# A selective-scan loop in a fixed order, and its output products as seven block products

## The chip, the cores and the metric

The kernel runs on one core of a Trainium2 chip. The metric is the device time of one execution in microseconds (us). A core has five engines with a queue each: TensorE (PE in the profile; its weight loads are listed as PEld), VectorE (DVE), ScalarE (ACT), GpSimd (POOL) and SyncE (SP), which here issues the DMAs. Each engine works through its own queue in order and waits on semaphores for the others.

## The reference

One layer of three parts, each on a layer norm of a residual `x` of 16 x 32 tokens with 512 features: a graph attention on 3-d coordinates, a selective scan, and a feed-forward part with low-rank additions. The change lies in the scan, which, cut to what matters, is:

```python
h = x * rsqrt(mean(x * x) + EPS) * norm_w
proj = einsum('bsd,od->bso', h, in_proj_w)            # gate 8192, hBC 8192 + 2048, dt 128
gate, hBC, dt = ...
hBC = silu(causal_conv(hBC, conv_w, conv_b))          # four taps along the sequence
hid, B, C = ...                                       # 128 heads of 64, 8 groups of 128
dt = softplus(dt + dt_bias);  A = -exp(A_log)
# within one chunk: y[i] = sum_j (C[i] . B[j]) * exp(segsum(A * dt))[i, j] * (hid * dt)[j]
y = (Y_diag + Y_off) + Dp * hid
yg = y * silu(gate)
yg = yg * rsqrt(mean over the group's 1024 channels of yg * yg + EPS) * gnorm_w
out = residual + einsum('bsd,od->bso', yg, out_proj_w)
```

All tensors of the scan are f32.

## The kernel before, in words

Three functions run one after the other: `graph_part` (up to about 1340 us of the span), `scan_part`, and `ffn_part` (from about 2276 us). Only `scan_part` is touched.

The 512 tokens lie along the free axis in four blocks of 128 (index q), channels along the partitions. The 8192 inner channels are 64 tiles of 128 (index t), eight per group (TG = 8), in 8 groups (G_M = 8). For a group g:

- `inner(g)` makes, for each of eight tiles i, the gate projection (`project`, L1177: four 512-column matmuls on `hT`, into the PSUM tag "p" with two buffers), its Silu on ScalarE (L1256, tile `gs`), the convolution projection, and `convolve`: an Identity on ScalarE that applies the last tap and the bias (L1184, tile `cy`), three taps on VectorE that read the same PSUM buffer (L1189), and the Silu into `hid` (L1192). From group 1 on it also advances `parts`, the loading and splitting of the low-rank weights of the feed-forward part into three bf16 parts (L148 to L185: masks and memsets on GpSimd, small DMAs, eight VectorE operations for each of ten pieces).
- `mix(g)` takes each tile i back to token-major order with four transposes (`pht`, L1285, PSUM tag "m", two buffers), multiplies by dt (`hd`, L1287), builds two decay matrices (`el`, L1298), multiplies on TensorE (`py`, L1306, PSUM tag "y"), adds `Dp * hid` (L1310), gates (L1311), squares on ScalarE (`ssq`, `sq`, L1313 and L1316), sums the squares on GpSimd (L1317), and scales by `gnorm_w` on ScalarE (L1318). For every second tile `decays` makes the decays of four heads: a product on GpSimd (`da`, L1265, two buffers), a matmul (`pl`, L1270, PSUM tag "m"), an Exp (`ed`, L1275).
- `close(g)` sums the squares over the group with a matmul (`pn`, L1325), takes the reciprocal root (`rstd`, L70 to L80, two ScalarE operations with other function tables), loads eight tiles of `out_proj` (`wo`, L1333, ten buffers), and for each q accumulates eight 128 x 128 x 512 matmuls (`po`, L1338, PSUM tag "o") and adds them, times the root, to the residual `xt` (L1341).

The source calls `inner(g + 1)`, `mix(g)`, `close(g)` in this order, but a scheduler decides the order on each engine: it takes instructions by priority as soon as their inputs and buffers are free. So the projections of group g + 1, the mix of g and the products of g and of the group before it are interleaved in small pieces.

An f32 matmul is two passes in the profile, each with a weight load of its own; a transpose is one pass.

Of the kernel before, what the change touches and what calls it, by code (L numbers as in the profile page):

```python
# [8 lines left out]
F32 = mybir.dt.float32  # L9
# [3 lines left out]
AF = mybir.ActivationFunctionType  # L13
ALU = mybir.AluOpType
# [4 lines left out]
P = 128  # L19
B = 16  # L20
C = 32
D = 512
# [9 lines left out]
CB = 3  # L32
# [8 lines left out]
H_M, G_M, SEQ = 128, 8, 32  # L41
D_INNER = 8192
NT = D_INNER // P
TG = NT // G_M
# [85 lines left out]
class LowRank:  # L130
# [981 lines left out]
def scan_part(nc, tc, cx, I, id32, ones, xt, u, rstd, lows):  # L1112
# [3 lines left out]
    wk = cx.enter_context(tc.tile_pool(name="swk", bufs=2))  # L1116
    sm = cx.enter_context(tc.tile_pool(name="ssm", bufs=3))
    wpool = cx.enter_context(tc.tile_pool(name="sw", bufs=4))
    ps_p = cx.enter_context(tc.tile_pool(name="sps_p", bufs=2, space=PSUM))
    ps_m = cx.enter_context(tc.tile_pool(name="sps_m", bufs=2, space=PSUM))  # L1120
    ps_y = cx.enter_context(tc.tile_pool(name="sps_y", bufs=2, space=PSUM))
    ps_o = cx.enter_context(tc.tile_pool(name="sps_o", bufs=2, space=PSUM))
# [23 lines left out]
    for t, base, cmul, op, b2, c2, s2 in ((le, 0, -1, ALU.is_ge, 0, 1, -32), (gt, 0, 1, ALU.is_gt, 31, -1, 32)):  # L1146
        nc.gpsimd.memset(t, 1.0)
        nc.gpsimd.affine_select(
            out=t, in_=t, compare_op=op, fill=0.0, base=base, pattern=[[-cmul, P]], channel_multiplier=cmul
        )  # L1150
        nc.gpsimd.affine_select(
            out=t, in_=t, compare_op=ALU.is_ge, fill=0.0, base=b2, pattern=[[s2, 4], [0, 32]], channel_multiplier=c2
# [10 lines left out]
    for q in range(4):  # L1163
        pt = ps_m.tile([P, 4, P], F32, tag="m", name=f"pt{q}")
# [6 lines left out]
    def project(t, tag):  # L1171

        w = wpool.tile([P, 4, P], F32, tag="win", name=f"win{tag}", bufs=6)
        nc.sync.dma_start(out=w, in_=I["in_proj"][t])
        pp = ps_p.tile([P, D], F32, tag="p", name=f"pp{tag}")
        for k in range(4):
            nc.tensor.matmul(pp, lhsT=w[:, k], rhs=hT[:, k], start=(k == 0), stop=(k == 3))  # L1177
        return pp

    def convolve(dst, t, tag):  # L1180

        pp = project(NT + t, f"c{tag}")
        y = wk.tile([P, B, SEQ], F32, tag="cy", name=f"cy{tag}", bufs=3)
        nc.scalar.activation(  # L1184
            y.rearrange("p b s -> p (b s)"), pp, AF.Identity, bias=cb[:, t:t + 1], scale=cw[:, t, 3:4]
        )
        pv = pp.rearrange("p (b s) -> p b s", b=B)
        for sh in (1, 2, 3):
            nc.vector.scalar_tensor_tensor(  # L1189
                y[:, :, sh:], pv[:, :, :SEQ - sh], cw[:, t, 3 - sh:4 - sh], y[:, :, sh:], ALU.mult, ALU.add  # L1190
            )
        nc.scalar.activation(dst, y.rearrange("p b s -> p (b s)"), AF.Silu)  # L1192


    wdt = wpool.tile([P, 4, P], F32, tag="win", name="wdt", bufs=6)
# [9 lines left out]
    with tc.tile_pool(name="soft", bufs=1) as sp:  # L1205
# [11 lines left out]
        s2 = sp.tile([P, 4, H_M], F32, name="s2")  # L1217
        nc.vector.tensor_tensor(s2, s, s, ALU.mult)
        acc = sp.tile([P, 4, H_M], F32, name="acc")
# [12 lines left out]
    CB = sc.tile([P, G_M, 4, P], F32, name="CB")  # L1232
# [13 lines left out]
    parts = lows.load(low)  # L1246
    big = cx.enter_context(tc.tile_pool(name="sbig", bufs=2))

    def inner(g):

        gs = big.tile([P, TG, D], F32, tag="gs", name=f"gs{g}")
        hid = big.tile([P, TG, D], F32, tag="hid", name=f"hid{g}")
        for i in range(TG):
            t = g * TG + i
            pg = project(t, f"g{t}")
            nc.scalar.activation(gs[:, i], pg, AF.Silu)  # L1256
            convolve(hid[:, i], t, f"h{t}")
            if g > 0:
                next(parts, None)
        return gs, hid  # L1260

    def decays(h):

        da = sm.tile([P, 4, 4, SEQ], F32, tag="da", name=f"da{h}", bufs=2)
        nc.gpsimd.tensor_tensor(  # L1265
            da, lei.unsqueeze(1).unsqueeze(1).to_broadcast([P, 4, 4, SEQ]),
            dA[:, :, h:h + 4].rearrange("p q h -> p h q").unsqueeze(3).to_broadcast([P, 4, 4, SEQ]), ALU.mult,
        )
        pl = ps_m.tile([P, 4, 4, SEQ], F32, tag="m", name=f"pl{h}")
        nc.tensor.matmul(  # L1270
            pl.rearrange("p h q i -> p (h q i)"), lhsT=gt, rhs=da.rearrange("p h q i -> p (h q i)"),
            start=True, stop=True,
        )
        ed = sm.tile([P, 4, 4, SEQ], F32, tag="ed", name=f"ed{h}", bufs=2)
        nc.scalar.activation(ed, pl, AF.Exp)  # L1275
        return ed

    def mix(g, gs, hid):

        ssq = wk.tile([P, D], F32, tag="ssq", name=f"ssq{g}")  # L1280
        for i in range(TG):
            t = g * TG + i
            pt = ps_m.tile([P, 4, P], F32, tag="m", name=f"pht{t}")
            for q in range(4):
                nc.tensor.transpose(pt[:, q], hid[:, i, q * P:(q + 1) * P], id32)  # L1285
            hd = sm.tile([P, 4, 2, 64], F32, tag="hd", name=f"hd{t}")
            nc.vector.tensor_tensor(  # L1287
                hd, pt.rearrange("p q (h c) -> p q h c", h=2),
                dt[:, :, 2 * t:2 * t + 2].unsqueeze(3).to_broadcast([P, 4, 2, 64]), ALU.mult,
            )  # L1290
            py = ps_y.tile([P, 4, P], F32, tag="y", name=f"py{t}")
            if i % 2 == 0:
                decay = decays(2 * t)
            els = []
            for j in range(2):

                el = sm.tile([P, 4, P], F32, tag="el", name=f"el{2 * t + j}")
                nc.vector.tensor_tensor(  # L1298
                    el.rearrange("p q (b i) -> p q b i", b=4),
                    decay[:, 2 * (i % 2) + j].unsqueeze(2).to_broadcast([P, 4, 4, SEQ]),  # L1300
                    CB[:, g].rearrange("p q (b i) -> p q b i", b=4), ALU.mult,
                )
                els.append(el)
            for q in range(4):
                for j in range(2):
                    nc.tensor.matmul(  # L1306
                        py[64 * j:64 * j + 64, q], lhsT=hd[:, q, j], rhs=els[j][:, q], start=True, stop=True
                    )
            pyf = py.rearrange("p q t -> p (q t)")
            nc.vector.scalar_tensor_tensor(hid[:, i], hid[:, i], dpc[:, t:t + 1], pyf, ALU.mult, ALU.add)  # L1310
            nc.vector.tensor_tensor(gs[:, i], gs[:, i], hid[:, i], ALU.mult)  # L1311
            if i == 0:
                nc.scalar.activation(ssq, gs[:, i], AF.Square)  # L1313
            else:
                sq = wk.tile([P, D], F32, tag="sq", name=f"sq{t}")
                nc.scalar.activation(sq, gs[:, i], AF.Square)  # L1316
                nc.gpsimd.tensor_tensor(ssq, ssq, sq, ALU.add)  # L1317
            nc.scalar.activation(gs[:, i], gs[:, i], AF.Copy, scale=gnw[:, t:t + 1])  # L1318
        return ssq

    def close(g, gs, ssq):

        pn = ps_y.tile([P, 4], F32, tag="y", name=f"pn{g}")
        for q in range(4):
            nc.tensor.matmul(pn[:, q:q + 1], lhsT=ssq[:, q * P:(q + 1) * P], rhs=ones[:, 0:1], start=True, stop=True)  # L1325
        mean = sm.tile([P, 4], F32, tag="gm", name=f"gm{g}")
        nc.vector.tensor_scalar(mean, pn, 1.0 / (TG * P), None, ALU.mult)
        rs = sm.tile([P, 4], F32, tag="gr", name=f"gr{g}")
        rstd(sm, rs, mean, 4, f"gn{g}")
        wo = []  # L1330
        for i in range(TG):
            w = wpool.tile([P, D], F32, tag="wo", name=f"wo{g}_{i}", bufs=TG + 2)
            nc.sync.dma_start(out=w, in_=I["out_proj"][g * TG + i])  # L1333
            wo.append(w)
        for q in range(4):
            po = ps_o.tile([P, D], F32, tag="o", name=f"po{g}_{q}")
            for i in range(TG):
                nc.tensor.matmul(  # L1338
                    po, lhsT=gs[:, i, q * P:(q + 1) * P], rhs=wo[i], start=(i == 0), stop=(i == TG - 1)
                )  # L1340
            nc.vector.scalar_tensor_tensor(xt[:, q], po, rs[:, q:q + 1], xt[:, q], ALU.mult, ALU.add)  # L1341

    cur = inner(0)
    for g in range(G_M):
        nxt = inner(g + 1) if g + 1 < G_M else None
        ssq = mix(g, *cur)
        close(g, cur[0], ssq)
        cur = nxt


def ffn_part(nc, tc, cx, I, id32, xt, layernorm, lows, out):
# [139 lines left out]
```

## Time and profile before

| what | value |
|---|---|
| median of 3 runs | 2381.26 us (2378.29 to 2382.47) |
| the profiled execution | 2376.64 us, span of its instructions 2374.9 us |
| TensorE matmul busy | 2172.0 us (91%), 39234 passes |
| TensorE weight loads busy | 1243.6 us (52%) |
| VectorE busy | 1694.5 us (71%) |
| ScalarE busy | 1093.6 us (46%) |
| GpSimd busy | 831.4 us (35%) |
| mean granted clock of TensorE | 0.978 |
| first gate projection, last output product | 1424.3 us, 2274.7 us |

The strips of the page cut the span into 40 slices of 59.4 us; a digit is the busy share in tenths. The scan's main loop fills slices 25 to 39. A row of the profile names the line, the engine, the operation, the tile written and the tiles read.

### The profile page before, as it was taken

To read this page: it belongs to the slowest core of one execution; us is meant where nothing else is said; L and a number is where in the kernel's file an instruction comes from. 1 tells how busy PE (TensorE), PEld (TensorE's weight loads), DVE (VectorE), ACT (ScalarE), POOL (GpSimd) and SP (SyncE) were. 2 spreads that over 40 slices of the span, in tenths; PEclk is the share of its full clock that TensorE was granted. 3 is DMA by queue.
4 is the path that set the end of the run, shared out by engine and by line. 5 is a ranking of instruction groups with operands and counts; after the bars stand their busy time and mean duration, and the time that the engine had idled before them with its cause. 6 is when DMAs were issued, how large, how long until landed. Compare 5 with 4: busy or idle time off the path is not lost. (4 is left out here: it accounts for less than half of the span.)

```text
span 2374.9 us, 88834 instructions
## 1 busy us (share of the span) xinstructions
PE 2172.0 (91%) x39234; PEld 1243.6 (52%) x39234; DVE 1694.5 (71%) x3674; ACT 1093.6 (46%) x2023; POOL 831.4 (35%) x897
## 2 busy tenths in 40 slices
PE   5598899999989988799999689999999999999979
PEld 2254555776547765477777444444444444444422
DVE  8487897998979999799899757455362635446543
ACT  6685666556755544355555233233242423333321
POOL 2155656556555566555555100021120202012200
PEclk9899999999999999999999799999999999999989
DMA  1323242231231412313111212212212031220000
GB/s 49 81 59 76 51 81 57 52 81 43 59 78 42 90 41 55 81 43 85 43 39 41 94 56 79 72 53 58 67 40 84 23 102 49 63 62 14 27 36 18
DMA packets 121625, 137.99 MB, mean 58 GB/s; under 512 B 18398, under 2 KB 79506, under 8 KB 121154
## 3 DMA queue, kind: packets, MB, share of 16 engines
q1 hardware_dynamic: 121240, 132.32, 22.6%
q8 instruction: 308, 5.05, 0.9%
q14 instruction: 77, 0.63, 0.1%
HBM read 77.02 MB, written 12.85 MB: 38 GB/s over the span
## 5 line engine op out<-in xcount | busy, mean ns | idle before, releaser
L888 POOL TENSOR_TENSOR EN<-e,rz 128x480 f32<-128x480 f32 x344 | 342.4, 995 | 509.6 <-DVE rz L886 423.1
L913 PE MATMUL u<-WA,DD 128*32 128x128 bf16 (+1 forms) x16512 | 412.5, 248 | 19.4 <-issue 19.1
L918 ACT COPY us<-u 128x512 f32<-128x512 f32 x516 | 301.9, 586 | 154.2 <-PE u L913 138.2
L913 PEld LDWEIGHTS <-DD 128*32 128x32 f16 x16512 | 337.5, 97 | 53.5 <-issue 51.1
L873 ACT ACTIVATE e<-s,smc 128x480 f32<-128x480 f32 x344 | 227.3, 661 | 270.2 <-PE s L868 243.5
L809 POOL TENSOR_TENSOR DD<-fs,crep 128x480 f16<-128x480 f32 (+2 forms) x344 | 349.4, 1016 | 0.0
L941 PE MATMUL h<-e,us 128*32 128x30 f32 (+1 forms) x11008 | 281.3, 210 | 47.1 <-DVE e L894 25.6
L941 PEld LDWEIGHTS h<-e,us 128*32 128x32 f32 (+1 forms) x11008 | 247.2, 125 | 147.0 <-issue 68.1
L1189 DVE SCALAR_TENSOR_TENSOR cyh<-ppch,t_conv_w,cyh 128x496 f32<-128x496 f32 (+2 forms) x192 | 137.5, 716 | 221.9 <-ACT cyh L1184 217.9
L860 DVE TENSOR_REDUCE c<-s 128x16 bf16<-128x480 f32 x344 | 220.0, 640 | 77.0 <-PE s L851 73.9
L1265 POOL TENSOR_TENSOR da<-lei,dA 128x512 f32<-128x512 f32 x32 | 40.6, 1269 | 612.6 <-PE pl L1270 577.6
L1338 PE MATMUL po<-wo,gs 128*128 128x512 f32 x512 | 240.5, 605 | 10.4 <-DVE xt L1341 10.3
L1177 PE MATMUL ppch<-hT,winch 128*128 128x512 f32 x512 | 232.2, 593 | 0.0
L1177 PE MATMUL ppg<-hT,wing 128*128 128x512 f32 x512 | 231.9, 593 | 0.0
L894 DVE STREAM_TRANSPOSE e<-EN 128x512 f32<-128x512 f32 x344 | 224.5, 653 | 0.0
L880 DVE TENSOR_REDUCE z<-e 128x16 f32<-128x480 f32 x344 | 219.4, 638 | 0.4 <-ACT e L873 0.4
L541 ACT ACTIVATE sgn<-kd 128x512 bf16<-128x512 f32 x256 | 153.1, 598 | 48.6 <-PE kd L540 45.7
L851 PEld LDWEIGHTS <-DD 128*32 128x32 f16 x5504 | 80.8, 96 | 156.8 <-issue 131.6
L751 DVE TENSOR_SCALAR oh<-it,rank 128x512 bf16<-128x512 f16 x512 | 156.6, 366 | 7.6 <-PE pp L705 7.5
L1177 PEld LDWEIGHTS ppch<-hT,winch 128*128 128x128 f32 x512 | 93.6, 190 | 122.7 <-issue 122.4
L851 PE MATMUL s<-DX,DD 128*32 128x120 f16 x5504 | 141.5, 222 | 16.9 <-DMA DX<-DD 15.7
L1177 PEld LDWEIGHTS ppg<-hT,wing 128*128 128x128 f32 x512 | 95.8, 190 | 114.0 <-issue 114.0
(327 smaller groups left out, 2845.5 us busy)
## 6 DMA issues: line engine op xcount, KB each, us to landing
DX<-DD SPq DMA_DIRECT2D x456, 90.0 KB
wo<-in_out_proj SPq DMA_DIRECT2D x64, 256.0 KB
wing<-in_in_proj SPq DMA_DIRECT2D x64, 256.0 KB
winch<-in_in_proj SPq DMA_DIRECT2D x64, 256.0 KB
crep<-dC SPq DMA_DIRECT2D x128, 64.0 KB
dS<-so SPq DMA_DIRECT2D x32, 256.0 KB
fs<-dS SPq DMA_DIRECT2D x128, 64.0 KB
wincB<-in_in_proj SPq DMA_DIRECT2D x8, 256.0 KB
```

The source lines that it names most:

```text
L809: nc.gpsimd.tensor_tensor(d[:, :, m0 - n0:n1 - n0], win, crep[:, :, m0:n1].unsqueeze(3).to_broadcast([P, 4, n1 - m0, K]), ALU.subtract,)
L851: nc.tensor.matmul(s[rh, j * 4 * QB:(j + 1) * 4 * QB].rearrange("p (b q) -> p b q", b=4), lhsT=d[:, h, c0:c0 + 32], rhs=dx[:, h, :, c0:c0 ...
L860: nc.vector.tensor_reduce(c, live["s", at, gi].rearrange("p (i q) -> p i q", q=QB), AX.X, ALU.max, negate=True)
L873: nc.scalar.activation(e, s.rearrange("p (i q) -> p i q", q=QB), AF.Exp, scale=smc)
L880: nc.vector.tensor_reduce(z, e, AX.X, ALU.add)
L888: nc.gpsimd.tensor_tensor(en[:, :, :QB], e, rz.unsqueeze(2).to_broadcast([P, NI, QB]), ALU.mult)
L894: nc.vector.transpose(e.rearrange("p i q -> p (i q)"), en.rearrange("p i q -> p (i q)"))
L913: nc.tensor.matmul(u[rh, jj], lhsT=d[:, h, c0:c0 + 32], rhs=WA[k][:, h].rearrange("p b o -> p (b o)"), start=(jj == 0 and k == 0), stop=(k ...
L918: nc.scalar.copy(us[:, j - jj:j + 1], u)
L941: nc.tensor.matmul(h[r:r + co, pr, q0:q0 + QB], lhsT=us[:, j, b * co:(b + 1) * co], rhs=e[:, 4 * j + b, :QB], start=npair > 1, stop=True, ...
L1177: nc.tensor.matmul(pp, lhsT=w[:, k], rhs=hT[:, k], start=(k == 0), stop=(k == 3))
L1338: nc.tensor.matmul(po, lhsT=gs[:, i, q * P:(q + 1) * P], rhs=wo[i], start=(i == 0), stop=(i == TG - 1))
```

## The change

The main loop's instructions now stand, on every engine, in the order in which the source issues them (`tc.manual_schedule()`). `inner`, `mix` and `close` are cut into steps for that: `gate`, `current` (the convolution, in two halves), and a class `Mix` with `turn` (transposes, `hd`, `el`, and the load of one `wo` tile), `outputs` (`py`), `gated` (gating, squares, their sum, scaling) and `summed`. Per tile i of a group: the gate projection of group g + 1; the second half of tile i - 1's convolution; `gated` of tile i - 1; `turn`, which in odd iterations also makes the next decays (`ahead`, with one `da` buffer in place of two); the convolution projection; the next sums, if any; `py`. The eight `wo` tiles of a group are loaded one per iteration, with eight buffers in place of ten.

In groups 0 to 5 the output products are computed by the seven-product scheme for 2 x 2 blocks (fifteen additions). A pair of channel tiles and two halves of a token block pair give 2 x 2 blocks of 128 x 128; two halves of the output give 2 x 2 blocks of 128 x 256. `operands` makes the sums on VectorE, in place where a block is used up; `close_by_seven` accumulates the seven products over the four pairs in seven half banks of PSUM, for each half of the tokens, and combines them on VectorE. Groups 6 and 7 keep the eight products; those of group 6 are issued during group 7's iterations.

The built program has 63 more TensorE rows (of the form in which one f32 matmul counts once), 300 more on VectorE, 12 more copies and 38 more table loads on ScalarE, and the same 900 on GpSimd.

```diff
-    def convolve(dst, t, tag):
+    def convolve_steps(dst, t, tag):
...
             y.rearrange("p b s -> p (b s)"), pp, AF.Identity, bias=cb[:, t:t + 1], scale=cw[:, t, 3:4]
         )
+        yield
...
+    cx.enter_context(tc.manual_schedule())
+    made = {}
+
+    def gate(g, i):
...
+        pg = project(g * TG + i, f"g{g * TG + i}")
+        nc.scalar.activation(made[g][0][:, i], pg, AF.Silu)
+
+    def current(g, i):
+        t = g * TG + i
+        yield from convolve_steps(made[g][1][:, i], t, f"h{t}")
+        if g > 0:
+            next(parts, None)
 
     def decays(h):
 
-        da = sm.tile([P, 4, 4, SEQ], F32, tag="da", name=f"da{h}", bufs=2)
+        da = sm.tile([P, 4, 4, SEQ], F32, tag="da", name=f"da{h}", bufs=1)
...
+        def turn(self, i):
...
             for q in range(4):
-                nc.tensor.transpose(pt[:, q], hid[:, i, q * P:(q + 1) * P], id32)
-            hd = sm.tile([P, 4, 2, 64], F32, tag="hd", name=f"hd{t}")
+                nc.tensor.transpose(pt[:, q], self.hid[:, i, q * P:(q + 1) * P], id32)
+            if i % 2:
+                ahead(2 * t + 2)
+            hd = sm.tile([P, 4, 2, 64], F32, tag="hd", name=f"hd{t}", bufs=2)
...
+            w = wpool.tile([P, D], F32, tag="wo", name=f"wo{t}", bufs=TG)
+            nc.sync.dma_start(out=w, in_=I["out_proj"][t])
...
+        def summed(self, i):
+
+            if self.g + 2 >= G_M:
+                return
+            if self.sums is None and i % 2 == 0 and i:
+                self.sums = operands(self.g, i // 2 - 1, self.gs, self.wo)
...
+    def operands(g, p, gs, wo):
...
+        nc.vector.tensor_tensor(t1, b12, b11, ALU.subtract)
+        nc.vector.tensor_tensor(t2, b22, t1, ALU.subtract)
+        nc.vector.tensor_tensor(b12, b22, b12, ALU.subtract)
+        nc.vector.tensor_tensor(t4, b21, t2, ALU.subtract)
+        yield
+        nc.vector.tensor_tensor(s1, a21, a22, ALU.add)
+        nc.vector.tensor_tensor(s2, s1, a11, ALU.subtract)
+        nc.vector.tensor_tensor(a21, a11, a21, ALU.subtract)
+        nc.vector.tensor_tensor(s4, a12, s2, ALU.subtract)
+        yield [(a11, b11), (a12, b21), (s4, b22), (a22, t4), (s1, t1), (s2, t2), (a21, b12)]
+
+    def close_by_seven(g, gs, ssq, wo, pairs):
...
+        for h in range(2):
+
+            banks = [
+                pool.tile([P, 2, HN], F32, tag=tag, name=f"po{g}_{h}_{tag}{k}")
+                for pool, tag in (((ps_p, "p"), (ps_m, "m")), ((ps_o, "o"), (ps_y, "y")))[h]
+                for k in range(2)
+            ]
+            acc = [banks[k // 2][:, k % 2] for k in range(7)]
+            for p, products in enumerate(pairs):
+                for k, (x, y) in enumerate(products):
+                    nc.tensor.matmul(
+                        acc[k], lhsT=x[:, h], rhs=y, start=(p == 0 and k % 2 == 0), stop=(p == TG // 2 - 1),
+                        skip_group_check=True,
+                    )
+                yield
+            if h == 0:
+                rs = root(g, ssq)
...
+            nc.scalar.copy(c, p1)
+            nc.vector.tensor_tensor(u2, c, p6, ALU.add)
...
-    cur = inner(0)
+    for i in range(TG):
+        gate(0, i)
+        end_of(current(0, i))
+    ahead(0)
+    last = None
     for g in range(G_M):
...
+        mix = Mix(g)
+        conv = None
+        for i in range(TG):
+            if g + 1 < G_M:
+                gate(g + 1, i)
+            end_of(conv)
+            conv = None
+            if i:
+                mix.gated(i - 1)
+            mix.turn(i)
+            if g + 1 < G_M:
+                conv = current(g + 1, i)
+                next(conv)
+            else:
+                next(last, None)
+            mix.summed(i)
+            mix.outputs(i)
+        end_of(conv)
+        mix.gated(TG - 1)
+        for _ in range(2):
+            mix.summed(TG)
+        end_of(last)
+        last = mix.closing()
+        if g + 2 != G_M:
+            end_of(last)
+            last = None
```

In the changed kernel the lines are L1261 (Silu of the gate), L1190 (taps), L1193 (Silu into `hid`), L1272 (`da`), L1277 (`pl`), L1282 (Exp), L1307 (`pht`), L1339 (`py`), L1354 (Square), L1355 (sum of the squares) and L1425 (the seven products).

More of the change, by code (lines that the diff above doesn't have):

```diff
@@ L1192, in convolve @@
         nc.scalar.activation(dst, y.rearrange("p b s -> p (b s)"), AF.Silu)
+    def convolve(*args):
+        for _ in convolve_steps(*args):
+            pass
     wdt = wpool.tile([P, 4, P], F32, tag="win", name="wdt", bufs=6)
@@ L1247, in scan_part @@
     big = cx.enter_context(tc.tile_pool(name="sbig", bufs=2))
[L1249 to L1260, printed above, removed]
+    cx.enter_context(tc.manual_schedule())
+    made = {}
+    def gate(g, i):
+        if i == 0:
+            made[g] = [big.tile([P, TG, D], F32, tag=n, name=f"{n}{g}") for n in ("gs", "hid")]
+        pg = project(g * TG + i, f"g{g * TG + i}")
[5 more added lines that the diff above has]
+            next(parts, None)
     def decays(h):
-        da = sm.tile([P, 4, 4, SEQ], F32, tag="da", name=f"da{h}", bufs=2)
+        da = sm.tile([P, 4, 4, SEQ], F32, tag="da", name=f"da{h}", bufs=1)
         nc.gpsimd.tensor_tensor(
@@ L1276, in decays, with ahead, __init__ @@
         return ed
[L1278 to L1282, printed above, removed]
+    decay = {}
+    def ahead(h):
+        if h < H_M:
+            decay[h] = decays(h)
+    class Mix:
+        def __init__(self, g):
+            self.g = g
+            self.gs, self.hid = made.pop(g)
+            self.ssq = wk.tile([P, D], F32, tag="ssq", name=f"ssq{g}")
+            self.wo = []
+            self.pairs = []
+            self.sums = None
+        def turn(self, i):
+            t = self.g * TG + i
             pt = ps_m.tile([P, 4, P], F32, tag="m", name=f"pht{t}")
             for q in range(4):
-                nc.tensor.transpose(pt[:, q], hid[:, i, q * P:(q + 1) * P], id32)
-            hd = sm.tile([P, 4, 2, 64], F32, tag="hd", name=f"hd{t}")
+                nc.tensor.transpose(pt[:, q], self.hid[:, i, q * P:(q + 1) * P], id32)
+            if i % 2:
+                ahead(2 * t + 2)
+            hd = sm.tile([P, 4, 2, 64], F32, tag="hd", name=f"hd{t}", bufs=2)
             nc.vector.tensor_tensor(
@@ L1290, in mix, with outputs @@
             )
-            py = ps_y.tile([P, 4, P], F32, tag="y", name=f"py{t}")
-            if i % 2 == 0:
-                decay = decays(2 * t)
             els = []
+            h0 = 4 * (t // 2)
             for j in range(2):
-                el = sm.tile([P, 4, P], F32, tag="el", name=f"el{2 * t + j}")
+                el = sm.tile([P, 4, P], F32, tag="el", name=f"el{2 * t + j}", bufs=2)
                 nc.vector.tensor_tensor(
                     el.rearrange("p q (b i) -> p q b i", b=4),
-                    decay[:, 2 * (i % 2) + j].unsqueeze(2).to_broadcast([P, 4, 4, SEQ]),
-                    CB[:, g].rearrange("p q (b i) -> p q b i", b=4), ALU.mult,
+                    decay[h0][:, 2 * (i % 2) + j].unsqueeze(2).to_broadcast([P, 4, 4, SEQ]),
+                    CB[:, self.g].rearrange("p q (b i) -> p q b i", b=4), ALU.mult,
                 )
                 els.append(el)
+            if i % 2:
+                decay.pop(h0)
+            self.now = hd, els
+            w = wpool.tile([P, D], F32, tag="wo", name=f"wo{t}", bufs=TG)
+            nc.sync.dma_start(out=w, in_=I["out_proj"][t])
+            self.wo.append(w)
+        def outputs(self, i):
+            t = self.g * TG + i
+            hd, els = self.now
+            py = ps_y.tile([P, 4, P], F32, tag="y", name=f"py{t}")
             for q in range(4):
@@ L1308, in mix, with gated @@
                     )
-            pyf = py.rearrange("p q t -> p (q t)")
+            self.py = py
+        def gated(self, i):
+            t = self.g * TG + i
+            gs, hid, ssq = self.gs, self.hid, self.ssq
+            pyf = self.py.rearrange("p q t -> p (q t)")
             nc.vector.scalar_tensor_tensor(hid[:, i], hid[:, i], dpc[:, t:t + 1], pyf, ALU.mult, ALU.add)
@@ L1318, in mix, with closing, root @@
             nc.scalar.activation(gs[:, i], gs[:, i], AF.Copy, scale=gnw[:, t:t + 1])
-        return ssq
-    def close(g, gs, ssq):
+        def summed(self, i):
[3 more added lines that the diff above has]
+                self.sums = operands(self.g, i // 2 - 1, self.gs, self.wo)
+            if self.sums:
+                got = next(self.sums)
+                if got:
+                    self.pairs.append(got)
+                    self.sums = None
+        def closing(self):
+            return (close_by_seven if self.g + 2 < G_M else close)(self.g, self.gs, self.ssq, self.wo, self.pairs)
+    def root(g, ssq):
         pn = ps_y.tile([P, 4], F32, tag="y", name=f"pn{g}")
@@ L1329, in close, with tokens @@
         rstd(sm, rs, mean, 4, f"gn{g}")
[L1330 to L1334, printed above, removed]
+        return rs
+    HN = D // 2
+    def tokens(gs, i, r):
+        return gs[:, i].rearrange("p (a r t) -> p r a t", a=2, r=2)[:, r]
+    def operands(g, p, gs, wo):
+        i0, i1 = 2 * p, 2 * p + 1
+        a11, a21, a12, a22 = (tokens(gs, i, r) for i in (i0, i1) for r in (0, 1))
+        S = sm.tile([P, 3, 2, P], F32, tag="osum", name=f"osum{g}_{p}", bufs=TG // 2)
+        s1, s2, s4 = (S[:, k] for k in range(3))
+        b11, b12, b21, b22 = (w[:, k * HN:(k + 1) * HN] for w in (wo[i0], wo[i1]) for k in (0, 1))
+        T = sm.tile([P, 3, HN], F32, tag="wsum", name=f"wsum{g}_{p}", bufs=TG // 2)
+        t1, t2, t4 = (T[:, k] for k in range(3))
+        nc.vector.tensor_tensor(t1, b12, b11, ALU.subtract)
[8 more added lines that the diff above has]
+        yield [(a11, b11), (a12, b21), (s4, b22), (a22, t4), (s1, t1), (s2, t2), (a21, b12)]
@@ new lines, in close_by_seven, with add_to @@
+    def close_by_seven(g, gs, ssq, wo, pairs):
+        acc = []
+        for h in range(2):
[14 more added lines that the diff above has]
+                rs = root(g, ssq)
+            p1, p2, p3, p4, p5, p6, p7 = acc
+            t0, t1 = (wk.tile([P, D], F32, tag="sq", name=f"ou{g}_{h}_{k}") for k in range(2))
+            u2, u3, c = t0[:, :HN], t0[:, HN:], t1[:, :HN]
+            def add_to(q, half, v):
+                x = xt[:, 2 * h + q, half * HN:(half + 1) * HN]
+                nc.vector.scalar_tensor_tensor(x, v, rs[:, 2 * h + q:2 * h + q + 1], x, ALU.mult, ALU.add)
+            nc.scalar.copy(c, p1)
+            nc.vector.tensor_tensor(u2, c, p6, ALU.add)
+            nc.vector.tensor_tensor(c, c, p2, ALU.add)
+            add_to(0, 0, c)
+            nc.vector.tensor_tensor(u3, u2, p7, ALU.add)
+            nc.vector.tensor_tensor(u2, u2, p5, ALU.add)
+            nc.vector.tensor_tensor(u2, u2, p3, ALU.add)
+            add_to(0, 1, u2)
+            nc.vector.tensor_tensor(c, u3, p4, ALU.add)
+            add_to(1, 0, c)
+            nc.vector.tensor_tensor(u3, u3, p5, ALU.add)
+            add_to(1, 1, u3)
@@ L1335, in close @@
+    def close(g, gs, ssq, wo, pairs):
         for q in range(4):
@@ L1340, in close, with end_of @@
                 )
+                if i == TG // 2 - 1:
+                    yield
+            if q == 0:
+                rs = root(g, ssq)
             nc.vector.scalar_tensor_tensor(xt[:, q], po, rs[:, q:q + 1], xt[:, q], ALU.mult, ALU.add)
-    cur = inner(0)
-    for g in range(G_M):
[L1345 to L1348, printed above, removed]
+            yield
+    def end_of(c):
+        for _ in c or ():
+            pass
+    for i in range(TG):
[3 more added lines that the diff above has]
+    last = None
+    for g in range(G_M):
+        mix = Mix(g)
[24 more added lines that the diff above has]
+            last = None
 def ffn_part(nc, tc, cx, I, id32, xt, layernorm, lows, out):
```

## The prediction

> **What bounds the kernel now.** I read the page's strips first, then the main loop's windows, then the busiest TensorE rows, then the rows of every operation that stands on the new order's path. Time is in us from the start of the span.
>
> ```profile
> PE   5598899999989988799999689999999999999979
> ```
>
> ```profile
> 1428.00:2276.00 848.00, 829.11 (x2944) 386.46 (x2943) 433.37 (x675) 286.40 (x412) 119.09 (x92) 1.00 0.19 55
> ```
>
> The first is the page's strip of TensorE's busy tenths, the second an answer of the windows view: from the first convolution projection to the last output product, 848 us, with TensorE (first number) busy 829.1, VectorE 433.4, ScalarE 286.4, GpSimd 119.1, and the clock at 1.00. So the main loop is TensorE's, idle there is 848.0 - 829.1 = 18.9, and every new wait of TensorE is paid in full unless it fits into that.
>
> Prices of TensorE passes, from the timeline (start, time to the last end, line, tile, passes; an f32 matmul is two passes):
>
> ```profile
> 1424.33 3.60 PE L1177 MATMUL ppg<-hT,wing 128*128 128x512 f32 x8
> 1427.76 1.09 PE L1177 MATMUL ppch<-hT,winch 128*128 128x512 f32 x2
> 1428.69 1.05 PE L1242 MATMUL pcb<-Cg,Bg 128*128 128x128 f32 x8
> 1429.58 2.74 PE L1177 MATMUL ppch<-hT,winch 128*128 128x512 f32 x6
> ```
>
> Eight 512-column passes take 1427.76 - 1424.33 = 3.43, or 0.429 each; eight 128-column ones 0.89, or 0.111 each, a quarter and a little, although each loads 128x128 weights. A pass's end stands 0.16 behind the next one's start (3.60 - 3.43).
>
> Durations of what the new order puts in a row (min/median/max in ns):
>
> ```profile
> L1256 ACT ACTIVATE gs<-ppg x64: 577/579/597, 1429.8 to 2162.7; 128x512 f32<-128x512 f32 x64
> ...
> L1192 ACT ACTIVATE hid<-cyh x64: 613/629/630, 1435.5 to 2171.7; 128x512 f32<-128x512 f32 x64
> ...
> L1316 ACT ACTIVATE sq<-gs x56: 622/630/632, 1546.5 to 2254.7; 128x512 f32<-128x512 f32 x56
> ...
> L1317 POOL TENSOR_TENSOR ssq<-ssq,sq x56: 1262/1463/1753, 1547.3 to 2255.5; 128x512 f32<-128x512 f32 x56
> ...
> L1265 POOL TENSOR_TENSOR da<-lei,dA x32: 1071/1248/1627, 1370.8 to 2226.8; 128x512 f32<-128x512 f32 x32
> ...
>   PE pl L1270: 577.6, 22
> ```
>
> The last line, under the row of da, says that GpSimd sat 577.6 us until a pl matmul had freed a da buffer: before, da is always made long ahead, and TensorE never waits for it.
>
> **The products.** Per group, 64 passes of 512 columns become 2 halves x 4 pairs x 7 products x 2 = 112 passes of 256. At half of 0.429 that is 112 x 0.2145 = 24.0 against 27.5; six groups save 20.6. The 256-column pass isn't in this form in the trace; it lies between the 128- and the 512-column rows, which both hide their weight load, so I take the interpolation. If each pass showed a seam of 0.07, as the two passes ahead of pcb do together (1428.69 - 1427.76 = 0.93 where 0.86 is due), 672 x 0.07 = 47 would be lost beside the saving; the 128-column row speaks against it. The extra sums cost VectorE 192 additions and some 130 operations on 256 columns, net about 116 us at 0.41 (estimated from 0.684 at 512 and 0.505 at 344 columns). An iteration then holds 3 x 0.72 + 0.74 + 0.68 x 4 + 4 x 0.41 = 7.3 of VectorE beside 9 of TensorE, so these are hidden; without that cover they would be 116.
>
> **The order.** In place of the scheduler's mixture each iteration issues on TensorE: gate projection (8 passes), 4 transposes pht, in odd iterations the two pl passes, convolution projection (8), 16 py passes. Most of the 18.9 idle (the page's groups have 10.4 of it in front of po) comes from the old mixture; fewer switches between tiles, at about 0.07 each, save a little more. I take -24, with bounds -10 and -30.
>
> **The wait that it adds.** In odd iteration i the built program has, on GpSimd, the ssq addition of i-1 ahead of da, and da has one buffer and is made in the same iteration in which pl uses it. The ssq addition waits for the Square of i-1; on ScalarE that stands behind the Silu of gate i, then the Silu of hid i-1; and the Silu of gate i waits for TensorE's gate projection, which is only just finished when TensorE reaches pl. With 0 at the gate's first pass:
> TensorE: gate ends 3.43 (its last result 3.59), transposes end 3.97, pl is next.
> ScalarE: 3.64 start; + 0.58 + 0.63 + 0.63 and two handovers = 5.53. VectorE is earlier: the last convolution ends at -1.1 (py follows it), Identity 0.78, three taps of 0.72, then 0.74 and 0.68 for hid and gs, and handovers: 3.5.
> GpSimd: 5.60 + 1.46 = 7.06, + 1.25 = 8.33. TensorE: 8.39.
> So TensorE stands 8.4 - 4.0 = 4.4 at pl (3.8 with all minima, 5.2 with all maxima), and behind pl are queued the convolution projection, py, and all later work. Nothing covers it: TensorE's next work is behind the wait in its own queue.
> How often: iteration 1 has no ssq addition in front; 3, 5 and 7 have. Groups 1 to 6: 18 x 4.4 = 79.2. Group 0 also has the low-rank split (8 VectorE operations, 3.4 per iteration, medians of L167 to L173) between taps and gating, which moves the chain by 2.3: 3 x 6.7, some 1.0 in each of three even iterations, and iteration 1, where GpSimd's memsets of the low-rank tiles (4.6 in all, done at 1331 to 1336 before, now started behind the taps) stand ahead of da: 4.9. Together 28. Group 1's last splits add 2.5. Group 7 has no gate, but pht is short and the chain runs from py: 0.2 + 0.74 + 0.68 + 0.63 + 1.46 + 1.25 and handovers = 5.2 against 0.6, twice: 9.3. Closing: the third product of a half needs the buffer of the last convolution, whose taps end 2.0 after py, against 0.9: 1.2 x 6 = 7.2. Sum of waits +126, in 24 stops of 4 to 7 us (105 with the minima and no wait at the closing, 145 with the maxima).
>
> ScalarE loads its function tables 38 times more, 1.283 each in the rows of L1256 and L1275: 49 in all. Once it is the load for Exp, which runs while ScalarE waits for pl, once that for Silu, which is over before the gate projection ends; so nothing on the path, and 49 if I am wrong there.
>
> The DMA queue also changes: on SP each wo load now stands between two projection loads and waits for the previous group's products. Six win buffers keep it three iterations ahead, so I price it at nothing; uncovered, a late load would cost a few us per group.
>
> **The clock.** The trace shows what follows a stop of that length, first in TensorE's timeline, then in windows:
>
> ```profile
> 1378.39 2.04 PE L1177 MATMUL ppcC<-hT,wincC 128*128 128x512 f32 x2 [3.97 <-issue]
> ```
>
> ```profile
> 1378.40:1383.70 5.30, 5.30 (x13) 3.23 (x14) 1.20 (x2) 1.25 (x2) 0.00 (x0) 0.50 0.00 0
> 1383.70:1390.00 6.30, 6.30 (x18) 2.89 (x17) 2.15 (x3) 2.06 (x3) 0.00 (x0) 1.00 0.15 42
> ...
> 431.40:434.80 3.40, 3.40 (x62) 2.14 (x62) 2.47 (x5) 0.79 (x2) 0.87 (x1) 0.50 0.06 21
> ...
> 835.10:842.00 6.90, 6.61 (x201) 5.32 (x202) 6.80 (x15) 3.11 (x6) 5.09 (x6) 1.00 0.14 31
> ```
>
> After 3.97 without work the granted clock (third number from the end) is 0.50 for 5.3 busy us, so 2.65 are lost; after a gap of 2.43 at 427.6 it is 0.50 for 3.4, 1.7 lost; a gap of 2.56 at 832.5 left it at 1.00 in the 6.9 that followed. All 24 stops are worked out as longer than 3.97, so I count 2.3 for each: +55, with bounds 0 and 24 x 2.7 = 65.
>
> The Trainium skill, page "TensorE: Matmul & The Clock Gate", section "HAM oscillation — how this bites in real kernels", warns only of idle gaps above about 3.4 us, counted in free-running windows of that length. Taken strictly, a 4.4 gap holds a whole window in 1.0 of 3.4 cases, so 7 of 24 stops would lose 1.7 each, 12 instead of 55, and the sum would be 2472 (an estimate from that page). The drop after 2.43 us speaks for the larger number.
>
> **Sum.** The profiled execution took 2376.6 (span 2374.9), 4.6 less than the median of 2381.3. 2376.6 - 20.6 - 24 + 126 + 55 = 2513; against the median I say 2515. What lies outside the loop keeps its instructions and I count it at 0.
>
> **The rivals.**
> Slower, but the clock stays up: 2515 - 55 = 2460. For it: the 2.56 gap. Against: the 3.97 one.
> Faster: da comes early, because the chain is short or overlaps in a way that I don't see, and the stops vanish: 2376.6 - 45 + 7 (closing) = 2339. It decides if the stop at pl is below (45 - 7) / 24 = 1.6 us each. For it: GpSimd's idle of 577.6 shows that da itself needs little. Against: even with all minima the chain gives 3.8, and the built order has no freedom.
> The products don't pay, from exposed weight loads at 256 columns: 2515 + 47 = 2562 with the stops, and 2339 + 47 = 2386 without them, where a seam of 0.07 is the point from which the products alone turn the change slower. Against: the 0.111 pass.
>
> **How the numbers follow.** 0.72 for the forecast, whose own range is 2480 to 2555 (waits 105 to 145, clock 41 to 65, not all at one end); 0.16 for the slower case without the clock (2435 to 2480); 0.07 for faster; 0.04 for exposed loads; 0.01 for a sum within 0.2%, about what a measurement here can tell from no change. The range 2440 to 2555 holds the first two nearly whole. Faster 0.07, same 0.01, slower 0.92.
>
> **What would show it.** Right: TensorE idle in front of pl of about 100 us with GpSimd's da as releaser, ssq waiting for Square and Square behind the two Silus; clock strips of 7 and 8 inside the loop; product passes 0.21 to 0.22 apart; a group period near 120 in place of 105 (the same po gap stands at 1891.64 and 1996.70 in the timeline of before). Wrong: pl without idle, or a releaser other than da; the clock at 1.00 through the loop; product passes of 0.3.

## The result, and the profile after

| | before | changed |
|---|---|---|
| median of four runs | 2381.32 us (2378.29 to 2382.47) | 2488.26 us (2483.20 to 2490.43) |
| ratio | | 1.0448, interval 1.0429 to 1.0467 |
| span of the profiled execution | 2374.9 us | 2487.3 us |

The change makes the kernel 4.5% slower; 2515 was predicted, with a range of 2440 to 2555.

The page's strips of the changed kernel, TensorE's busy tenths and its granted clock:

```profile
PE   5697999999989988899996997888898989798779
PEclk9899999999989999999998998899999999999989
```

The windows view, from the same instruction of the loop as before to the end of its last product (busy us of TensorE, its weight loads, VectorE, ScalarE and GpSimd, then clock, DMA share, GB/s):

```profile
1428.00:2388.50 960.50, 833.05 (x3232) 457.87 (x3230) 576.68 (x975) 333.07 (x462) 132.13 (x99) 0.95 0.16 52
```

The loop takes 960.5 in place of 848.0 us, so all of the span's 112.4 more lie here. TensorE has 3232 passes in it where 2944 stood, 288 more, which is just what the products add (672 for 384), or 144 f32 matmuls; the 63 rows named under the change don't fit that. TensorE's idle time rose from 18.9 to 960.5 - 833.1 = 127.5, and the clock fell from 1.00 to 0.95. The waits view of the same stretch (who waited for whom, us, times, longest) and a group of the page (busy, mean ns, idle in front and its releaser) say where the idle time stands:

```profile
POOL ssq L1355 <- ACT sq L1354: 740.1, 56, 43.2
...
PE pl L1277 <- POOL da L1272: 109.4, 25, 6.7
```

```profile
L1277 PE MATMUL pl<-da,gt 128*128 128x512 f32 x64 | 57.6, 998 | 109.4 <-POOL da L1272 109.4
```

The same row in the loop before:

```profile
L1270 PE MATMUL pl<-da,gt 128*128 128x512 f32 x64 | 34.3, 618 | 0.0
```

109.4 of the 127.5 us stand in front of one pair of passes, pl, which never waited before. Its row also has a mean of 998 ns where 618 stood: it runs at the lowered clock. One stop in TensorE's timeline, then ScalarE's and GpSimd's of the same time (an idle time in brackets is followed by what ended it):

```profile
1907.83 3.70 PE L1177 MATMUL ppg<-hT,wing 128*128 128x512 f32 x8
1911.36 0.60 PE L1307 MATMUL pht<-id,hid 128*128 128x128 f32 x4
1916.28 2.08 PE L1277 MATMUL pl<-da,gt 128*128 128x512 f32 x2 [4.32 <-POOL da L1272]
1918.15 4.11 PE L1177 MATMUL ppch<-hT,winch 128*128 128x512 f32 x8
```

```profile
1911.56 0.60 ACT L1261 ACTIVATE gs<-ppg 128x512 f32<-128x512 f32 x1 [3.88 <-PE ppg L1177]
1912.06 0.62 ACT L1193 ACTIVATE hid<-cyh 128x512 f32<-128x512 f32 x1
1912.58 0.62 ACT L1354 ACTIVATE sq<-gs 128x512 f32<-128x512 f32 x1
...
1913.97 1.28 ACT L1282 ACT_TABLE_LOAD   x1
```

```profile
1913.62 1.39 POOL L1355 TENSOR_TENSOR ssq<-ssq,sq 128x512 f32<-128x512 f32 x1 [7.14 <-ACT sq L1354]
1914.98 1.25 POOL L1272 TENSOR_TENSOR da<-lei,dA 128x512 f32<-128x512 f32 x1
```

Read from top to bottom: the gate projection ends, its Silu starts (1911.56), then the Silu of hid, the Square, the addition of the squares, da, and at 1916.28 pl. Every link starts within some 0.4 us of the end of the one in front, and TensorE does nothing from 1911.96 on. There are 24 such stops. The same place in the windows view, for the clock (third number from the end):

```profile
1915.80:1916.30 0.50, 0.02 (x1) 0.02 (x1) 0.50 (x1) 0.00 (x0) 0.43 (x1) 0.50 0.00 0
1916.30:1919.20 2.90, 2.90 (x4) 1.35 (x5) 0.88 (x3) 0.60 (x1) 0.00 (x0) 0.51 0.00 0
1919.20:1925.00 5.80, 5.80 (x28) 2.75 (x27) 1.82 (x3) 2.06 (x2) 0.00 (x0) 1.00 0.00 0
```

The clock drops 3.8 us after the stop began, half a us before it ends, and stays at half for 3.4 us, so 1.4 us of work are lost. The clock's records put 102 us of the loop at 0.50, 88 of them with TensorE busy: 44 us lost. These are 26 stretches: one at each of the 24 stops, and two behind waits of 1.24 us in front of py.

The seven products, in the timeline, for their price:

```profile
1950.31 1.03 PE L1425 MATMUL po_m<-wsum,osum 128*128 128x256 f32 x4
1951.18 0.59 PE L1425 MATMUL po_m<-wo,gs 128*128 128x256 f32 x2
```

Four passes in 0.87 us, or 0.218 each; the median over all of them is 0.216, half of the 512-column pass.

### The profile page after: what moved, and what is told of

Its sections match the earlier page's. It is cut to its first block, busy times and chain, and to the rows that moved or that the text cites. A ratio compares the mean times of both kernels' runs of the same rounds, so it can differ in the third digit from the quotient of the medians.

```text
span 2487.3 us, 89748 instructions
## 1 busy us (share of the span) xinstructions
PE 2178.6 (88%) x39522; PEld 1317.0 (53%) x39522; DVE 1837.3 (74%) x3974; ACT 1141.0 (46%) x2073; POOL 839.2 (34%) x897
## 5 line engine op out<-in xcount | busy, mean ns | idle before, releaser
L1355 POOL TENSOR_TENSOR ssq<-ssq,sq 128x512 f32<-128x512 f32 x56 | 88.6, 1582 | 740.1 <-ACT sq L1354 740.1
L1190 DVE SCALAR_TENSOR_TENSOR cyh<-ppch,t_conv_w,cyh 128x496 f32<-128x496 f32 (+2 forms) x192 | 137.7, 717 | 223.4 <-ACT cyh L1184 218.9
L1177 PE MATMUL ppch<-hT,winch 128*128 128x512 f32 x512 | 246.9, 627 | 0.0
L1177 PE MATMUL ppg<-hT,wing 128*128 128x512 f32 x512 | 238.7, 609 | 0.0
L1177 PEld LDWEIGHTS ppch<-hT,winch 128*128 128x128 f32 x512 | 104.7, 210 | 130.7 <-issue 129.2
L1277 PE MATMUL pl<-da,gt 128*128 128x512 f32 x64 | 57.6, 998 | 109.4 <-POOL da L1272 109.4
```

## The experiments

The theory is that of the prediction: the stops come from the place of da behind the ssq addition in GpSimd's queue, the clock's loss comes from the stops, and without both the change would save time. The rivals are that pl waits for something else as well, that the clock falls for another reason, and that the sums eat what the products save. Each ratio is to runs of the kernel before that were taken beside the experiment's; their median was 2372.7 us for four experiments (da ahead of the ssq addition, the fixed order alone, the seven products in the scheduled order, pl behind the convolution projection) and 2380.5 for the other four. So times of different experiments are compared by their ratios.

### da ahead of the ssq addition

```diff
+    das = {}
+
+    def decay_input(h):
...
         nc.gpsimd.tensor_tensor(da, ...)
+        das[h] = da
...
         for i in range(TG):
+            if i % 2:
+                decay_input(2 * (g * TG + i) + 2)
             if g + 1 < G_M:
                 gate(g + 1, i)
```

`decays` takes the tile from `das`; all else stays, pl's place included.

> The changed kernel with GpSimd's da made at the start of the odd iteration, ahead of the ssq addition; the pl matmul stays where it is. Theory (TensorE stands at pl because da is queued behind the ssq addition, and the clock falls after each stop): the 108.9 us in front of pl and the clock's loss (44 us by the clock's rows) both go, and with less slack VectorE makes TensorE wait some 5 us more in groups 0 and 1: 2488 - 109 - 44 + 5 = 2340. Rival (the chain from Square is late for another reason, say pl's PSUM buffer or the Exp): the idle only changes its releaser, 2450 or more. Rival (the clock falls for another reason than the stops): 2488 - 109 = 2380.

Measured: 2341.25 us, ratio 0.9860 (0.9838 to 0.9883). The window of the loop and the row of pl:

```profile
1428.00:2243.40 815.40, 791.48 (x3236) 444.07 (x3235) 576.41 (x976) 333.14 (x462) 133.32 (x99) 0.99 0.19 61
```

```profile
L1288 PE MATMUL pl<-da,gt 128*128 128x512 f32 x64 | 33.5, 606 | 0.5 <-POOL da L1276 0.5
```

The 109.4 us in front of pl are 0.5, its mean is 606 ns again, and the clock is at 0.99. Moving one GpSimd instruction past another takes the loop, from its first convolution projection to its last product, from 960.8 to 813.8 us. The ratio falls from 1.0448 to 0.9860, which is 140 us, and the result is 1.4% ahead of the kernel before. (That the median meets the expected 2340 is in part luck: the runs of before were 8.6 us faster here; at the ratio it would be 2348.) So the stops and the clock's loss have the cause that was named.

### The fixed order alone

```diff
-            if self.g + 2 >= G_M:
-                return
+            return
...
-            return (close_by_seven if self.g + 2 < G_M else close)(self.g, ...)
+            return close(self.g, ...)
```

> As e1_da_early, but all eight groups use the eight products (no sums, no combining), so what remains of the change is the fixed order alone. Theory: 672 passes of 256 columns become 384 of 512, 20.6 us more than e1_da_early, less the closing waits of 6.8: about 2340 + 14 to 20 = 2357. Rival (the sums and the combining on VectorE cost what the passes save): the same time as e1_da_early, 2340, or less.

Measured: 2355.21 us, ratio 0.9925 (0.9902 to 0.9948), to the same runs of before as the one above. The fixed order without stops is worth 0.75% of the time; the seven products are worth another 0.65%, some 14 us, after paying their closing waits of 7.2. In the two profiled executions the loop, from its first convolution projection to its last product, takes 824.3 us here and 813.8 with the seven products. TensorE's busy time, counted at the full clock, is 802.1 here and 785.0 there, 17 less, but its idle time is 13.6 here and 23.9 there: 7.2 of these 10 are the closing waits, 5 more stand in front of py. So the sums and the combining on VectorE, and the waits for buffers, eat part of the saving and not all of it.

### The seven products in the scheduled order

In the kernel before, `close(g)` of groups 0 to 5 calls `operands` and `close_by_seven` in place of its loop; `el` and `hd` have two buffers, `da` one, `wo` eight, since the sums need the room.

> The kernel before, in its scheduled order, with the seven products in groups 0 to 5 (wo with eight buffers, da with one, hd and el with two, as in the changed kernel). Theory (the passes are saved in any order): 2381 - 20 = 2361, with 2350 to 2375 as bounds. Rival (the seven products hold the PSUM buffers of the projections and of the mix for a whole half, and the scheduler's mixture lived from these): no gain or a loss, 2381 to 2420.

Measured: 2407.51 us, ratio 1.0141 (1.0120 to 1.0162): 34 us slower than before. My theory missed here. Its window and the row of py:

```profile
1428.00:2308.00 880.00, 826.67 (x3236) 448.82 (x3234) 539.50 (x961) 291.02 (x424) 116.08 (x93) 0.99 0.17 54
```

```profile
L1306 PE MATMUL py<-el,hd 128*64 128x128 f32 x1024 | 98.3, 286 | 39.9 <-DVE el L1298 35.4 <-DVE hd L1287 3.3
```

TensorE's busy time hardly falls (826.7 against 829.1) and its idle time grows from 18.9 to 53.3, of which 39.9 in front of py (5.0 before), mostly released by VectorE's el. The time lies in the rival's range, but its reason, the PSUM buffers, isn't what this row shows. Two things changed at once, the buffers and the products; the next experiment parts them.

### The buffers alone

```diff
-        da = sm.tile(..., tag="da", ..., bufs=2)
+        da = sm.tile(..., tag="da", ..., bufs=1)
...
-            hd = sm.tile(..., tag="hd", ...)
+            hd = sm.tile(..., tag="hd", ..., bufs=2)
...
-                el = sm.tile(..., tag="el", ...)
+                el = sm.tile(..., tag="el", ..., bufs=2)
...
-            w = wpool.tile([P, D], F32, tag="wo", ..., bufs=TG + 2)
+            w = wpool.tile([P, D], F32, tag="wo", ..., bufs=TG)
```

> The kernel before with the fewer buffers that the seven products leave room for (el and hd two in place of three, da one, wo eight in place of ten), nothing else. Theory (in e3_scheduled_seven the products themselves disturb the scheduled order): within 5 of before, 2372 to 2382. Rival (the buffers that were given up cost what e3_scheduled_seven lost, since TensorE there waited 32 us at py): 2400.

Measured: 2394.01 us, ratio 1.0048 (1.0031 to 1.0065). Between the two: fewer buffers cost 0.5%, about 12 us, and the products in the scheduled order another 0.9%. The row of py here has 6.5 idle, so the 39.9 above belong to the products. That it is the sums and the combining on VectorE in front of el is argued from that row's releaser; no run took them away.

### pl behind the convolution projection

```diff
-            if i % 2:
-                ahead(2 * t + 2)
...
                 next(last, None)
+            if i % 2:
+                ahead(2 * (g * TG + i) + 2)
             mix.summed(i)
```

> The changed kernel with the decays (da, pl, Exp) issued behind the convolution projection in place of ahead of it; GpSimd's order is the same, so da is as late as before, but TensorE has 3.5 us of work in front of pl. Theory: da is ready 8.28 after the gate's first pass (3.97 + the 4.31 measured), pl is reached at 7.5, so each stop shrinks to about 0.8, in groups 0 and 1 to 1.5 to 3: 24 us in all; stops this short leave the clock up. 2488 - (109 - 24) - 42 = 2361. Rival (the clock falls after these too): 2400. Rival (what makes da late waits for TensorE's convolution as well): as the changed kernel, 2488.

Measured: 2355.04 us, ratio 0.9916 (0.9894 to 0.9938). The timeline of a late group:

```profile
1868.75 0.60 PE L1307 MATMUL pht<-id,hid 128*128 128x128 f32 x4
1869.19 3.60 PE L1177 MATMUL ppch<-hT,winch 128*128 128x512 f32 x8
1873.67 1.12 PE L1277 MATMUL pl<-da,gt 128*128 128x512 f32 x2 [0.88 <-POOL da L1272]
```

GpSimd's da comes no earlier, but 3.5 us of TensorE's work now stand in front of pl, and the stop is 0.88 in place of 4.32. All 24 add up to 29.7 us. None of the 20 stops of 0.6 to 1.4 us at pl was followed by a lower clock; three of the four longer ones, of 2.3 to 3.3 us in groups 0 and 1, were.

### Square ahead of the gate's Silu

```diff
-        nc.scalar.activation(made[g][0][:, i], pg, AF.Silu)
+        return lambda: nc.scalar.activation(made[g][0][:, i], pg, AF.Silu)
...
             if i:
                 mix.gated(i - 1)
+            if g + 1 < G_M:
+                silu()
```

> The changed kernel with the Silu of the gate issued behind the Square and the scaling of the tile before, so ScalarE no longer makes the Square wait for the gate projection; da stays behind the ssq addition. Theory: the Square then waits for VectorE's gating (done at 3.5 by the working) in place of ScalarE's turn (4.9), so the 18 stops of 4.3 in groups 1 to 6 become about 3.0, those of group 0, set by the low-rank split on VectorE, and of group 7 hardly change: 2488 - 18 x 1.3 = 2465, and less if stops of 3.0 sometimes leave the clock up (each drop is worth some 1.6): 2440 to 2465. Rival (ScalarE's order isn't on the path): 2488.

Measured: 2463.90 us, ratio 1.0361 (1.0324 to 1.0398). Three stops of one group, and two windows behind them:

```profile
1768.23 1.12 PE L1277 MATMUL pl<-da,gt 128*128 128x512 f32 x2 [3.13 <-POOL da L1272]
1791.23 2.08 PE L1277 MATMUL pl<-da,gt 128*128 128x512 f32 x2 [3.12 <-POOL da L1272]
1815.36 1.12 PE L1277 MATMUL pl<-da,gt 128*128 128x512 f32 x2 [3.13 <-POOL da L1272]
```

```profile
1769.70:1773.10 3.40, 3.40 (x6) 1.31 (x5) 0.49 (x2) 0.29 (x1) 0.00 (x0) 0.50 0.00 0
1815.40:1819.00 3.60, 3.60 (x9) 1.69 (x10) 1.89 (x5) 0.60 (x1) 0.00 (x0) 1.00 0.00 0
```

The stop is 3.1 where 3.0 was worked out, so ScalarE's order is a link of the chain. Two equal stops are followed by a clock of 0.50 and of 1.00: of the 17 stops of 3.0 to 3.4, nine dropped the clock. What decides is worked out in the last section.

### Two repairs on top

The first starts the first half's products in the banks of tag m; the second also advances the low-rank split in every second iteration only. Both on top of da ahead.

```diff
-                for pool, tag in (((ps_p, "p"), (ps_m, "m")), ((ps_o, "o"), (ps_y, "y")))[h]
+                for pool, tag in (((ps_m, "m"), (ps_p, "p")), ((ps_o, "o"), (ps_y, "y")))[h]
```

> As e1_da_early, with the first half's products started in the banks of tag m, so the buffer of the last convolution is needed for the seventh product in place of the third. Theory: the six closing waits (7.2 in e1_da_early) go: 2341 - 7 = 2334. Rival (another buffer of the m banks is late then, since the last transposes and the last decays sit there): the wait moves and the time stays at 2341.

Measured: 2339.55 us, ratio 0.9825 (0.9800 to 0.9849). The six closing waits fell from 7.2 to 1.7, which is the part of group 0, and the loop, from its first convolution projection to its last product, from 813.8 to 807.0. That is what was expected of it, but the two intervals of the timed ratios overlap (0.9838 to 0.9883 without it), so the gain stands on the traces.

```diff
-        if g > 0:
+        if g > 0 and i % 2 == 0:
             next(parts, None)
```

> As e7_banks, with one piece of the low-rank split in every second iteration (groups 0 to 2) in place of each. Theory: VectorE's load in an iteration of group 0 falls from 7.3 + 3.4 = 10.7, more than TensorE's 9, to 9 on average, and of the 15 us of waits at py in e1_da_early about 10 go: 2334 - 10 = 2324. Rival (TensorE waits there for the chain of one tile, not for VectorE's load): 2334, since the same pieces hold up the same number of tiles.

Measured: 2338.07 us, ratio 0.9814 (0.9791 to 0.9838). The rows of py, first without and then with this edit:

```profile
L1350 PE MATMUL py<-el,hd 128*64 128x128 f32 x1024 | 77.5, 284 | 14.7 <-DVE el L1331 14.5
```

```profile
L1350 PE MATMUL py<-el,hd 128*64 128x128 f32 x1024 | 77.0, 282 | 15.7 <-DVE el L1331 15.5
```

The waits at py stay at 15 us, and only spread over three groups: the rival was right. A piece of the split holds up the tile that it stands in front of, whatever VectorE's mean load is. This is the fastest version of the study, 1.9% ahead of the kernel before, but not told apart from the one above.

## Why the prediction was right, and which terms were off

**The stop.** Worked out as 4.4 in groups 1 to 6; the trace has 4.13 to 4.32, except for the first of group 1 (5.7, with the split), and 4.78 where 4.65 was said for group 7. The number, 24, is exact. Group 0 has 4.04, 5.05, 6.74 and 5.04 where 4.9 and three times 6.7 were said; the split moved the chain less than I had put. In all, idle of 109 at pl, 11 at py and 7 at the closing: 127.5 against 126. That the sum is so near is luck in part: the working gives 116 at pl (79.2, 25 of group 0, 2.5 and 9.3) and 3 at py, and the two misses cancel. The table loads, priced at nothing, cost nothing: the one in the stop shown starts behind the Square and the scaling, at 1913.97, and all of TensorE's idle time in the loop ends with da, el or the taps.

**The clock.** Each stop dropped it, as said. The term was mis-sized, 44 for 55: I took 2.3 us for each, from two gaps of other lengths; in this loop the half clock lasts one stretch of 3.4 us at 20 of the 24 stops and mostly starts before the stop ends, so these cost 1.4 to 1.7, the other four (two stretches each) 2.4 to 2.7. The strict reading of the Trainium skill ("TensorE: Matmul & The Clock Gate", "HAM oscillation — how this bites in real kernels"), 7 drops for 12 us, doesn't agree with 24 drops out of 24; the last section counts what does.

**The products.** 672 passes at 0.216 against 384 at 0.429 save 20 us; predicted 20.6. The fixed order with and without them differs by 17 in busy time. The exposed weight load, a rival, didn't show. (The seam from which it would have turned the change slower without stops is 38 us over 672 passes, or 0.056, and not 0.07, which already gives 2386.)

**The order.** This step failed in size: -24 was taken, with -30 as the bound. TensorE's busy time at the full clock is 833.1 - 44.0 = 789.0, 40 less than before. Of these 17 to 20 are the products, so 20 to 23 are left for the order; the fixed order alone, at 802.1, is 27 less than before. Most of it is py, whose 16 passes of a tile now stand together, first before and then changed:

```profile
L1306 PE MATMUL py<-el,hd 128*64 128x128 f32 x1024 | 90.6, 281 | 5.0 <-DVE el L1298 4.9
```

```profile
L1339 PE MATMUL py<-el,hd 128*64 128x128 f32 x1024 | 73.9, 279 | 11.0 <-DVE el L1320 10.8
```

That the seams between tiles are the reason is argued from these rows; no run changed the seams alone. With the old idle time of 18.9, all of which the new count of waits replaces, that is 39 at the least, 15 more than predicted. What I had called little, the switches between tiles, was as large as all of the old idle time.

The sum by what was measured: -20 - 39 + 127.5 + 44 = +112.5, as the window of the loop has it; it closes by construction, since the order's term is what the others leave. The two errors, 11 and 15, both made the forecast too slow. A third is in the last step: 2513 is for a profiled execution 4.6 us below the median, so the forecast against the median should have been 2517 or 2518 and not 2515.

**The rivals.** The slower one without the clock's fall (2460) is out by the clock rows. The faster one gave 2339 for a kernel without stops, 0.984 of the profiled execution before; da ahead of the ssq addition came to 0.986. Its point of decision, 1.6 us per stop, is borne out by pl behind the convolution projection: stops of 1.2 on average, and faster than before. Of the signs named, the clock's strip has 8 and 9 inside the loop and not 7 and 8, and a group takes 116 us (1832.15 to 1948.24, the same closing wait of two groups) for the 120 that were said, as both terms above were too slow.

## What to carry to other kernels

When a scheduler's order is replaced by one written by hand, follow for every instruction of the bottleneck engine what stands in front of its inputs in the other engines' queues, in the same iteration: an input that needs nothing can be late because of its neighbours. Make such an input one step earlier, or put independent work of the bottleneck engine in front of its use. A saving in operations may hang on the order: the seven products gained in the fixed order and lost in the scheduled one.

## What the runs showed of the hardware

Stops of 4.0 us and more lowered the clock 24 times in 24, stops of about 3.1 us nine times in 17. The length alone doesn't decide. In each trace all stretches of half clock begin on one raster of 3.41 us, to within 5 ns. Cut by this raster, the loops of the ten profiled executions have 2421 windows at the full clock. Of the 51 in which TensorE was idle for more than 0.58 of the window, every one was followed by half clock; of the 2316 below 0.395, none; of the 54 between, 14. A stop of 4.3 us puts at least 2.15 us, or 0.63, into one window wherever it falls. A stop of 3.1 us can be split evenly, 0.45 and 0.45, or lie in one window with 0.91, so its place decides, and short waits that fall into one window can do the same.

A VectorE operation whose two inputs both lie in SBUF stretches when it begins while a GpSimd addition or product runs. In the changed kernel's timeline, VectorE and GpSimd:

```profile
1929.19 1.49 DVE L1401 TENSOR_TENSOR wsum<-wo 128x256 f32<-128x256 f32 x1
1930.71 0.42 DVE L1402 TENSOR_TENSOR wsum<-wo,wsum 128x256 f32<-128x256 f32 x1
```

```profile
1928.72 1.68 POOL L1355 TENSOR_TENSOR ssq<-ssq,sq 128x512 f32<-128x512 f32 x1 [12.50 <-ACT sq L1354]
```

A subtraction of this shape takes 0.42 us alone and 1.49 when it begins under the addition, 0.28 beyond that one's end. Every one of the 24 first sums (L1406) and 14 of 24 of L1401 met one. Operations that read PSUM didn't stretch: 35 of L1310 in the kernel before began under a GpSimd operation and took their usual 0.74. Summed over the loop, the stretches are 36 us before and 68 in the changed kernel, which accounts for VectorE's loop time growing by 143 us where 116 were worked out. The Trainium skill says that GpSimd's SBUF interfaces are shared with VectorE, with contention for instructions of two SBUF inputs ("GPSIMD Engine Reference", "1. Specifications"); these rows agree and give it a size.
